# A fused attention layer on one core: the endings' rows read from chunk 12 on, and the shift rows' chain started two half steps earlier

## The chip, the core and the metric

The kernel runs on one core of a Trainium2 chip. The metric is device time in microseconds (us) of one execution. Engines are named as in the profile: PE (TensorE), ACT (ScalarE), DVE (VectorE), POOL (GpSimd), and SP (SyncE), which here does nothing but issue every DMA, in program order.

## What is computed

The input x has 8 batches of 2048 tokens with 512 channels, in float32. Cut to what matters:

```
xn   = layernorm(x)
q, k = heads of xn @ Wq.T + bq, xn @ Wk.T + bk       # 8 heads of 8
v    = heads of xn @ Wv.T + bv                       # 8 heads of 64
beta = softmax(leaky(q k^T / sqrt(8), 0.2))          # over 2048 keys
s    = gamma * (beta v) + xn
g    = silu(xn @ W.T + the low-rank term of the top expert)
out  = x + s * g
```

## The kernel before, in words

**Sequences, chunks, half steps.** A block is 512 tokens, so a batch has four blocks n, and the 8 heads make four pairs p. One sequence is one (batch, pair, block of queries): 16 sequences in a batch, 128 in all, with `b, p, n = s // 16, s % 4, (s % 16) // 4`. A sequence goes through 16 chunks of 128 keys. The double loop over s and i in the main part is written out by hand, and one pass of it is called a half step here and written (s,i); there are 2048. In the trace a half step begins with its first matmul of `less_max` (L657).

**What a half step issues.** On PE: `less_max` for one head (L657), two score matmuls of the next chunk (L640), two matmuls of `max_unit` (L586), `less_max` for the other head; then what the scheduler gives, mostly `weigh` (L681) of earlier chunks. On ACT: two exponentials (L669) and two leaky steps (L651). On DVE: one max reduction of `max_unit`, L597, which frees the only PSUM buffer `mx` for the next half step's two L586. On POOL: one addition of exponentials, L701.

**Maxima and shift rows.** The softmax needs each query's maximum before the sequence starts. `max_unit` runs `CH + LEAD` half steps ahead: with LEAD = 9 the last unit of sequence s+1 is issued in (s,6), and the first unit of sequence s+2 in (s,7). After the last one `shift_rows` is put in a queue and goes on by one `yield` in each half step: a reduction m (L603, DVE) in (s,6); two tiny DVE operations big and m (L609, L610) and a chain of six tiny POOL operations (L611 to L616) in (s,7); the transpose cT (L621, DVE), four DMAs to SH (L623) and four DMAs back to the tile shift (L629) in (s,9). The tile is first used in (s+1,0).

**Stacks.** `load_stacks(s+2)`, called in (s,0) to (s,3), reads the keys and queries of sequence s+2: two DMAs `k` (L542) and two `q_sb` (L548). The three key buffers make the `k` DMA wait for the last scores of sequence s-1, so SP issues it around (s-1,13) to (s,0).

**Ending.** When the last values of sequence s have been weighed, `ending(s)` enters the queue: a copy avs (L708); a half step later the reads of the block's rows, gs (L714) and the two halves of xs (L716, L717); then three idle half steps, the denominators dps (L724, L732, L734, L736), the transposed values atp (L741, L743), the addition of xs (L744), and in the next half step L747, L748 and the write of the output (L749). The tiles `dps` and `atp` take the one PSUM buffer `m`, which the background work takes too.

**Background.** Between the `weigh` matmuls runs a list of tasks: `lift_block` of this batch (the gate g, written to GS at L520, after which the block is `lifted`), and `project_block` of the next batch (L338 to L390: eight writes of keys and queries of 128 KB, then XN and XT, 1 MB each). `norm` and `lift_block` have tiny POOL operations too (L309 to L313, L434, L435). In the last batch only `lift_block` is left, and `half_light` takes the place of `half_full`.

**Order.** All engines run their own instructions in program order. SP waits at a DMA until its source and buffer are free, and everything behind waits with it.

Of the kernel before, what the change touches and what calls it, by code (L numbers as in the profile page):

```python
# [8 lines left out]
FP = mybir.dt.float32  # L9
# [12 lines left out]
NT = BLK // 128  # L22
# [10 lines left out]
def fused_layer_kernel(  # L33
# [37 lines left out]
    nc = tc.nc  # L71
    B, M, C = x.shape
# [3 lines left out]
    SEQ = NPAIR * NB  # L76

    xv = x.rearrange("b (n p t) c -> b n p t c", p=128, t=NT)
# [5 lines left out]
    two = ctx.enter_context(tc.tile_pool(name="two", bufs=2))  # L84
# [12 lines left out]
    GS = [tc.dram_tile([NB, 128, NT, C], FP, name=f"GS{b}") for b in range(B)]  # L97
    XN = [tc.dram_tile([NB, 128, NT, C], FP, name=f"XN{b}") for b in range(B)]
# [110 lines left out]
    def set_up_ffn(ul):  # L209

        nc.vector.tensor_scalar_mul(w_sb, w_sb, 0.5)
        yield

        uh = one.tile([128, C], FP, name="hi")
        nc.vector.tensor_scalar_mul(ul, ul, 0.5)
        nc.vector.tensor_tensor(
            uh.bitcast(I32), ul.bitcast(I32), hi_bits.to_broadcast([128, C]), ALU.bitwise_and
        )
        nc.scalar.copy(wu_sb, uh)
        for g in (1, 3):  # L220
            r = slice(32 * g, 32 * g + 32)
            nc.vector.tensor_tensor(wu_sb[r, :], ul[r, :], uh[r, :], ALU.subtract)
# [21 lines left out]
    TINY, SLOW, WAIT, HOLD, FREE, IDLE = 5, 4, 3, 2, 1, 0  # L244
# [4 lines left out]
    def spend(cost):  # L249
        spent[0] += cost  # L250
# [44 lines left out]
    lifted = []  # L295
# [228 lines left out]
    def where(s):  # L524
        return s // SEQ, s % NPAIR, (s % SEQ) // NPAIR
# [28 lines left out]
    def load_values(s):  # L554
        if s >= B * SEQ:
            return
        b, p, n = where(s)
        while b not in valued:
            force()
        vts[s] = two.tile([128, CH, 128], FP, name="v_sb")  # L560
        nc.sync.dma_start(out=vts[s], in_=VS[b][p])
# [37 lines left out]
    def shift_rows(s):  # L599
        if s >= B * SEQ:  # L600
            return
        m = sm.tile([128, 2 * NT, 1], FP, name="m")
        nc.vector.reduce_max(m, mxr.pop(s).rearrange("p e t n -> p (e t) n"), axis=AX.X)  # L603
        yield IDLE

        ml = sm.tile([128, 2 * NT], FP, name="ml")
        c = parts[s % 2][:, 0 : 4 * NT].rearrange("p (i m) -> p i m", i=2)
        big = sm.tile([128, 2 * NT], FP, name="big")
        nc.vector.tensor_scalar(big, m[:, :, 0], 0.0, SLOPE, ALU.min, ALU.mult)  # L609
        nc.vector.tensor_scalar_max(m[:, :, 0], m[:, :, 0], 0.0)  # L610
        nc.gpsimd.tensor_tensor(ml, m[:, :, 0], big, ALU.add)  # L611
        nc.gpsimd.tensor_tensor(big, ml, splitter.to_broadcast([128, 2 * NT]), ALU.mult)
        nc.gpsimd.tensor_tensor(ml, ml, minus_one.to_broadcast([128, 2 * NT]), ALU.mult)
        nc.gpsimd.tensor_tensor(c[:, 1, :], big, ml, ALU.subtract)
        nc.gpsimd.tensor_tensor(c[:, 0, :], big, c[:, 1, :], ALU.subtract)
        nc.gpsimd.tensor_tensor(c[:, 1, :], ml, c[:, 0, :], ALU.subtract)  # L616
        for _ in range(2):
            yield IDLE

        cT = sm.tile([128, 32], FP, name="cT")  # L620
        nc.vector.transpose(cT, parts[s % 2])  # L621
        for q in range(4):
            nc.sync.dma_start(  # L623
                out=SH[s % 2][:, :, :, q, :].rearrange("i e t j -> (i e t) j"),
                in_=cT[32 * q : 32 * q + 4 * NT, :],
            )
        shift = qp.tile([128, BLK], FR, name="shift")
        for g in range(4):
            nc.sync.dma_start(  # L629
                out=shift[STK * g : STK * g + 2, :].bitcast(FP),  # L630
                in_=SH[s % 2][:, g % 2].rearrange("i t q j -> i (t q j)"),
            )
        shifts[s] = shift
# [19 lines left out]
    def less_max(s, i, sc, e):  # L653

        r = rows(i % 2, e)
        r = slice(r.start, r.start + 2)
        nc.tensor.matmul(  # L657
            sc[e],
            lhsT=ones_r[r, :],
            rhs=shifts[s][r, :],  # L660
            start=False,
            stop=True,
            skip_group_check=True,
        )
# [28 lines left out]
    def add_up(s, i, ex):  # L693
# [6 lines left out]
            acc[s] = two.tile([128, 2, BLK], FP, name="acc")  # L700
        nc.gpsimd.tensor_tensor(acc[s], old, ex, ALU.add)  # L701

    def ending(s):

        b, p, n = where(s)
        cols = slice(p * 128, (p + 1) * 128)
        avs = two.tile([128, BLK], FP, name="avs")
        nc.vector.tensor_copy(avs, avt.pop(s))  # L708
        yield IDLE
        sums = acc.pop(s)  # L710
        while (b, n) not in lifted:
            yield IDLE
        gs = two.tile([128, NT, 128], FP, name="gs")
        nc.sync.dma_start(out=gs, in_=GS[b][n][:, :, cols])  # L714
        xs = two.tile([128, 2, NT, 128], FP, name="xs")
        nc.sync.dma_start(out=xs[:, 0], in_=xv[b, n][:, :, cols])  # L716
        nc.sync.dma_start(out=xs[:, 1], in_=XN[b][n][:, :, cols])  # L717
        for _ in range(3):
            yield IDLE
        yield TINY  # L720

        dps = ps_m.tile([128, 2, NT, 32], FP, name="dps2", tag="m")
        for q in range(4):
            nc.tensor.matmul(  # L724
                dps[32 * q : 32 * q + 32],
                lhsT=ones[:, 0:32],
                rhs=sums.rearrange("p e (t q j) -> p e t q j", t=NT, q=4)[:, :, :, q, :],
                start=True,
                stop=True,
            )  # L730
        dv = dps.rearrange("p e t j -> p (e t) j")
        nc.vector.tensor_tensor(dv, dv, diag.unsqueeze(1).to_broadcast([128, 2 * NT, 32]), ALU.mult)  # L732
        rd = sm.tile([128, NT, 2, 1], FP, name="rd")
        nc.vector.reduce_sum(rd.rearrange("p t e o -> p e t o"), dps, axis=AX.X)  # L734
        rd = rd.rearrange("p t e o -> p (t e) o")
        nc.vector.reciprocal(rd, rd)  # L736
        spend(0.5)
        yield TINY
        tp = ps_m.tile([128, NT, 128], FP, name="atp", tag="m")
        for t in range(NT):  # L740
            nc.tensor.transpose(tp[:, t, :], avs[:, t * 128 : (t + 1) * 128], ident)  # L741
        tv = tp.rearrange("p t (e d) -> p (t e) d", e=2)
        nc.vector.tensor_tensor(tv, tv, rd.to_broadcast([128, NT * 2, DV]), ALU.mult)  # L743
        nc.vector.tensor_tensor(tp, tp, xs[:, 1], ALU.add)  # L744
        spend(0.5)
        yield WAIT
        nc.vector.tensor_tensor(tp, tp, gs, ALU.mult)  # L747
        nc.vector.tensor_tensor(gs, tp, xs[:, 0], ALU.add)  # L748
        nc.sync.dma_start(out=ov[b, n][:, :, cols], in_=gs)  # L749
# [25 lines left out]
    def due_at(h):  # L775
        w, t = h * END, 0.0
        for _, _, _, cost, end in tasks:
            w += cost * max(0.0, min(1.0, (h - t) / (end - t)))
            t = end
        return w  # L780
# [39 lines left out]
    def force():  # L820

        j = ahead()[0] if ahead() else 2
        go(j)
# [55 lines left out]

    MUCH, AHEAD = 3, 6.0  # L880

    LEAD = 9
    END = 1.0
    total = B * SEQ * CH

    with tc.manual_schedule():
# [110 lines left out]
        first, late = shift_rows(0), set_up_ffn(ul)  # L997
        units = [(0, u) for u in range(CH)] + [(1, u) for u in range(LEAD)]
        for n in range(1, NB):
# [30 lines left out]
        for s in range(B * SEQ):  # L1030
            for i in range(CH):
                if i <= 3 and s + 2 not in qst and (where(s + 2)[0] in (0, *ready) or i == 3):
                    load_stacks(s + 2)
                if i >= 6 and s + 1 not in vts and (where(s + 1)[0] in valued or i == 13):
                    load_values(s + 1)
                due[0] = due_at(s + (i + 1) / CH)
                u = s * CH + i + CH + LEAD
                nxt = s * CH + i + 1


                less_max(s, i, sc0, 0)
                if nxt < total:
                    sc1 = score(nxt // CH, nxt % CH)
                max_unit(u // CH, u % CH, flip=True)
                less_max(s, i, sc0, 1)
                if u % CH == CH - 1 and u < total:
                    queue[1], state[1] = shift_rows(u // CH), IDLE
                ex = exp(sc0)
                if nxt < total:
                    leaky(sc1)  # L1050
                if s < (B - 1) * SEQ:
                    half_full()
                else:
                    half_light()
                add_up(s, i, ex)
                last.append((s, i, ex))
                sc0 = sc1
        values(len(last))
        for _ in ending(B * SEQ - 1):
            pass  # L1060
# [44 lines left out]
```

## Time and profile before

| | |
|---|---|
| median of three runs | 5637.28 us (5630.33 to 5653.89) |
| the profiled execution's own time | 5619.18 us |
| its span, first to last instruction | 5617.4 us |
| first less_max matmul of (0,0) and of (127,15) | 131.2 us, 5598.6 us |
| busy share of the span: PE, POOL, ACT, DVE | 96%, 85%, 79%, 65% |
| granted PE clock, mean | 0.968 |

The span divides into 131 us before the loop, 5467 us of loop (2.67 us per half step) and 19 us after it. The length of a half step is read in the timeline as the distance between the first L657 matmuls of two half steps. Rows of a wait read: engine and line that waited, what it waited for, total us, times, longest us. The sums below are made against this execution.

### The profile page before, as it was taken

Reading aid. Unit: us, or ns where it says so; the run is one execution under the profiler, and the core shown is the slowest. Engines: PE = TensorE matmul, PEld = TensorE weight load, DVE = VectorE, ACT = ScalarE, POOL = GpSimd, SP = SyncE. Lnnn points to the kernel's source line nnn. Section 1 sums busy time; section 2 is a strip of 40 time slices with the busy share of each in tenths; the row PEclk is TensorE's granted clock in tenths of the full one; section 3 lists DMA queues with packets and bytes.
Section 4 is the critical chain, followed back from the end, with each engine's and each line's share of the span. In section 5 each row is a group of like instructions: output and inputs, shape, how many; then the busy total and the mean of one; then the engine's idle time right before and its main releaser. Section 6 shows DMA issues by size and latency. Waiting matters only on the chain.

```text
span 5617.4 us, 78032 instructions
## 1 busy us (share of the span) xinstructions
PE 5378.9 (96%) x26258; PEld 1999.1 (36%) x26258; DVE 3673.9 (65%) x4988; ACT 4440.7 (79%) x8627; POOL 4779.1 (85%) x2906
## 2 busy tenths in 40 slices
PE   8999999999999999999999999999999999999998
PEld 3333333333333333333333333333333333333332
DVE  5577666766676666667666666666766766645653
ACT  2788878888888878888788887888878888767777
POOL 1789988888888888888888888888888888878878
PEclk9999999999999999999999999999999999979989
DMA  5333432434324343252432434234343333322221
GB/s 197 106 112 121 128 113 88 128 106 147 104 78 142 93 146 95 76 158 91 142 92 83 147 112 130 80 111 131 107 123 99 102 120 122 100 78 78 71 63 61
DMA packets 528264, 615.38 MB, mean 110 GB/s; under 512 B 44092, under 2 KB 438332, under 8 KB 491768
## 3 DMA queue, kind: packets, MB, share of 16 engines
q1 hardware_dynamic: 527864, 610.39, 35.6%
q8 instruction: 209, 3.42, 0.3%
q14 instruction: 191, 1.56, 0.1%
HBM read 407.88 MB, written 202.38 MB: 109 GB/s over the span
## 4 chain that ended last, share of the span: by engine, by line
PE 80%; ACT 8%; DVE 7%; DMA 2%; issue 2%; SPq 1%; POOL 1%; POOLq 0%; ACTq 0%; DVEq 0%
PE av L681 28%; PE sc L657 16%; PE zps L279 9%; PE vps L279 8%; PE mx L586 7%; ACT ex L669 5%; ACT sc L651 2%; PE pps L265 2%; DVE mxr L597 2%; PE qkps L265 2%; PE dps L265 2%; PE dps L724 1%; DMA xs<-XN 1%; PE atp L741 1%; DVE gs L748 1%
## 5 line engine op out<-in xcount | busy, mean ns | idle before, releaser
L701 POOL TENSOR_TENSOR acc<-acc,ex 128x1024 f32<-128x1024 f32 x1792 | 4231.0, 2361 | 301.7 <-ACT ex L669 189.3
L597 DVE TENSOR_REDUCE mxr<-mx 128x2 f32<-128x1024 f32 x2032 | 2480.2, 1221 | 1260.0 <-PE sc L657 1018.5
L669 ACT ACTIVATE ex<-sc 128x512 f32<-128x512 f32 x4096 | 2231.0, 597 | 972.2 <-PE sc L657 829.0
L651 ACT ACTIVATE sc<-sc 128x512 f32<-128x512 f32 x4096 | 2237.7, 593 | 18.9 <-PE sc L640 18.9
L681 PE MATMUL av<-ex,v_sb 128*64 128x512 f32 x8192 | 2149.5, 630 | 11.6 <-DVE avs L708 9.2
L657 PE MATMUL sc<-shift,ones_r 2*128 2x512 f32 x4096 | 1679.7, 463 | 75.5 <-ACT sc L651 66.9
L586 PE MATMUL mx<-k,q_sb 32*128 32x512 f32 x4096 | 1445.4, 454 | 37.0 <-DVE mxr L597 35.9
L657 PEld LDWEIGHTS sc<-shift,ones_r 2*128 2x128 f32 x4096 | 703.6, 187 | 1560.4 <-ACT sc L651 1450.5
L640 PE MATMUL sc<-q_sb,k 32*128 32x512 f32 x4096 | 1037.4, 503 | 0.0
L681 PEld LDWEIGHTS av<-ex,v_sb 128*64 128x64 f32 x8192 | 469.7, 138 | 839.6 <-issue 805.2
L586 PEld LDWEIGHTS mx<-k,q_sb 32*128 32x128 f32 x4096 | 562.2, 188 | 61.2 <-DVE mxr L597 49.4
L279 PE MATMUL zps<-w_sb,xnT 128*128 128x512 f32 (+1 forms) x1120 | 541.0, 597 | 32.7 <-DMA xnT<-XT 14.1
L279 PE MATMUL vps<-wv_sb,xnT 128*128 128x512 f32 x960 | 475.2, 619 | 7.4 <-DVE gs L748 7.2
L701 POOL TENSOR_TENSOR acc<-ex 128x1024 f32<-128x1024 f32 x128 | 301.8, 2358 | 197.3 <-ACT ex L669 197.3
L640 PEld LDWEIGHTS sc<-q_sb,k 32*128 32x128 f32 x4096 | 385.9, 185 | 0.8 <-issue 0.8
L279 PEld LDWEIGHTS zps<-w_sb,xnT 128*128 128x128 f32 x1120 | 187.6, 192 | 270.3 <-issue 247.9
L279 PEld LDWEIGHTS vps<-wv_sb,xnT 128*128 128x128 f32 x960 | 164.0, 189 | 209.7 <-issue 195.9
L518 DVE SCALAR_TENSOR_TENSOR g<-th,zps 128x512 f32<-128x512 f32 x128 | 88.0, 688 | 189.2 <-ACT th L517 189.2
L611 POOL TENSOR_TENSOR ml<-m,big 128x8 f32<-128x8 f32 x128 | 26.2, 205 | 176.6 <-DVE m L610 176.6
L349 DVE TENSOR_TENSOR vb<-vps,bv_sb 128x512 f32<-128x512 f32 x120 | 83.0, 691 | 95.6 <-PE vps L279 95.4
L265 PE MATMUL dps<-xnT,wd_sb 128*128 128x512 f32 (+1 forms) x280 | 139.1, 607 | 0.0
L265 PE MATMUL pps<-xnT,wp_sb 128*128 128x512 f32 (+1 forms) x280 | 130.9, 585 | 5.0 <-DVE gs L748 5.0
(124 smaller groups left out, 2656.7 us busy)
## 6 DMA issues: line engine op xcount, KB each, us to landing
v_sb<-VS SPq DMA_DIRECT2D x127, 1024.0 KB
k<-KS SPq DMA_DIRECT2D x256, 256.0 KB
XN<-xn SPq DMA_DIRECT2D x32, 1024.0 KB
q_sb<-QS SPq DMA_DIRECT2D x256, 128.0 KB
xnT<-XT SPq DMA_DIRECT2D x32, 1024.0 KB
GS<-g SPq DMA_DIRECT2D x32, 1024.0 KB
gs<-GS SPq DMA_DIRECT2D x128, 256.0 KB
xs<-in_x_dram SPq DMA_DIRECT2D x128, 256.0 KB
```

What stands on the lines that cost most here:

```text
L265: nc.tensor.matmul(ps[:, part], lhsT=wt[:, c, :], rhs=xnT[c][:, part], start=(c == 0 and part.start == 0), stop=(c == NC - 1 and part.stop ...
L279: nc.tensor.matmul(ps[:, part], lhsT=xnT[c][:, t * 128 : (t + 1) * 128], rhs=wt[:, c, part], start=(c == 0 and part.start == 0), stop=(c = ...
L349: nc.vector.tensor_tensor(vb[:, :, t, :], ps.rearrange("p (h d) -> p h d", h=NPAIR), bv_sb.rearrange("p (h d) -> p h d", h=NPAIR), ALU.add,)
L518: nc.vector.scalar_tensor_tensor(g[:, t, :], th, 1.0, ps, ALU.add, ALU.mult)
L586: nc.tensor.matmul(parts[e], lhsT=q_sb[r, t * 128 : (t + 1) * 128], rhs=k_sb[r, kb // 2 * BLK : (kb // 2 + 1) * BLK], start=True, stop=True,)
L597: nc.vector.reduce_max(mxr[s][:, :, t, kb : kb + 1], mx, axis=AX.X)
L640: nc.tensor.matmul(sc[e], lhsT=k_sb[r, i // 2 * 128 : (i // 2 + 1) * 128], rhs=q_sb[r, :], start=True, stop=True,)
L651: nc.scalar.activation(sc[e], sc[e], AF.Prelu, alpha=SLOPE)
L657: nc.tensor.matmul(sc[e], lhsT=ones_r[r, :], rhs=shifts[s][r, :], start=False, stop=True, skip_group_check=True,)
L669: nc.scalar.activation(ex[:, e, :], sc[e], AF.Exp, scale=qscale)
L681: nc.tensor.matmul(avt[s][64 * e : 64 * e + DV, :], lhsT=v_sb[:, i, 64 * e : 64 * e + DV], rhs=ex[:, e, :], start=(i == 0), stop=(i == CH ...
L701: nc.gpsimd.tensor_tensor(acc[s], old, ex, ALU.add)
```

## The change

Four edits are made. The reads of an ending (L714 to L717) move into a function of their own, called at the head of the half steps (s,12) to (s,15) as soon as the block is lifted; the ending takes the tiles from it, and where they aren't there it calls the function itself, and idles one half step more than before. `shift_rows` idles four half steps instead of two between the POOL chain and the transpose. One more idle half step stands between the four DMAs to SH and the four back. LEAD is 11 instead of 9, so that all maxima, and with them the start of `shift_rows`, are issued two half steps earlier; before the loop two more units are issued, and the units end two half steps earlier in the last sequences.

```diff
@@ shift_rows
         nc.gpsimd.tensor_tensor(c[:, 1, :], ml, c[:, 0, :], ALU.subtract)
-        for _ in range(2):
+        for _ in range(4):
             yield IDLE
 
         cT = sm.tile([128, 32], FP, name="cT")
...
                 in_=cT[32 * q : 32 * q + 4 * NT, :],
             )
+        yield IDLE
         shift = qp.tile([128, BLK], FR, name="shift")
         for g in range(4):
             nc.sync.dma_start(
@@ new function, ahead of ending
+    reads = {}
+
+    def read_for_ending(s):
+
+        b, p, n = where(s)
+        if s >= B * SEQ or s in reads or (b, n) not in lifted:
+            return
+        cols = slice(p * 128, (p + 1) * 128)
+        gs = two.tile([128, NT, 128], FP, name="gs")
+        nc.sync.dma_start(out=gs, in_=GS[b][n][:, :, cols])
+        xs = two.tile([128, 2, NT, 128], FP, name="xs")
+        nc.sync.dma_start(out=xs[:, 0], in_=xv[b, n][:, :, cols])
+        nc.sync.dma_start(out=xs[:, 1], in_=XN[b][n][:, :, cols])
+        reads[s] = gs, xs
@@ ending
         sums = acc.pop(s)
-        while (b, n) not in lifted:
+        while s not in reads:
+            read_for_ending(s)
             yield IDLE
-        gs = two.tile([128, NT, 128], FP, name="gs")
-        nc.sync.dma_start(out=gs, in_=GS[b][n][:, :, cols])
-        xs = two.tile([128, 2, NT, 128], FP, name="xs")
-        nc.sync.dma_start(out=xs[:, 0], in_=xv[b, n][:, :, cols])
-        nc.sync.dma_start(out=xs[:, 1], in_=XN[b][n][:, :, cols])
+        gs, xs = reads.pop(s)
         for _ in range(3):
             yield IDLE
         yield TINY
@@ schedule
-    LEAD = 9
+    LEAD = 11
...
                     load_values(s + 1)
+                if i >= 12:
+                    read_for_ending(s)
                 due[0] = due_at(s + (i + 1) / CH)
```

## The prediction

> **What bounds the kernel now.** I read the page's busy shares and slices, the waits, the groups of L609, L621 and L744, and then the timeline where the waits cluster.
>
> ```profile
> PE 5378.9 (96%) x26258; PEld 1999.1 (36%) x26258; DVE 3673.9 (65%) x4988; ACT 4440.7 (79%) x8627; POOL 4779.1 (85%) x2906
> PEclk9999999999999999999999999999999999979989
> ```
>
> PE sets the pace: a usual half step is 2.58 us, in which POOL's addition takes 2.36. A gain must come from PE's idle time (240 us of the span) or from its clock (mean 0.968). Who makes PE idle:
>
> ```profile
> PE mx L586 <- DVE mxr L597: 35.9, 20, 3.7
> PE zps L279 <- DMA xnT<-XT: 14.1, 1, 14.1
> DVE atp L744 <- DMA xs<-XN: 25.9, 8, 4.0
> DVE cT L621 <- POOL c L616: 3.8, 1, 3.8
> ```
>
> The third row belongs to the first edit: DVE stood 25.9 us at xs, in 8 of 128 endings. The fourth belongs to the second: the transpose waited for POOL once in 128, in (126,9), where no more maxima are due. So longer idling ahead of it has nothing to save. One xs wait, in (61,8):
>
> ```profile
> 2747.37 0.49 PE L657 MATMUL sc<-shift,ones_r 2*128 2x512 f32 x1
> 2748.96 0.70 DVE L744 TENSOR_TENSOR atp<-atp,xs 128x512 f32<-128x512 f32 x1 [3.33 <-DMA xs<-XN]
> 2750.84 0.79 PE L586 MATMUL mx<-k,q_sb 32*128 32x512 f32 x2 [2.97 <-DVE mxr L597]
> 2751.99 3.68 PE L681 MATMUL av<-ex,v_sb 128*64 128x512 f32 x8
> 2755.60 0.79 PE L657 MATMUL sc<-shift,ones_r 2*128 2x512 f32 x1
> ```
>
> DVE waits 3.33 for xs, its max reduction queues behind, PE idles 2.97, and then eight L681 take 3.68 instead of the usual 1.94: the clock is halved. The half step lasts 8.23. Why xs is late shows in SP's timeline:
>
> ```profile
> 2731.57 1.28 SPq L338 DMA_DIRECT2D KS<-hi  x2
> 2737.90 0.45 SPq L390 DMA_DIRECT2D XT<-xnT  x1
> 2738.39 1.30 SPq L714 DMA_DIRECT2D gs<-GS  x1
> 2741.20 1.81 SPq L717 DMA_DIRECT2D xs<-XN  x1
> ```
>
> The reads sit in (61,4) behind the 3 MB that `project_block` wrote, and are used 7.8 us later. The same happens after sequences 12, 28, 44, 60, 76, 92 and 108; the eighth wait is 0.19.
>
> **Edit 1, the reads at (s,12).** No instruction is added, only SP's order changes. For these seven, block 3 is lifted by (10,14) of its batch, so SP meets the reads around (60,12), ahead of the stacks of (60,13) and of the writes of (61,2), and the data has twelve half steps, some 30 us, to land. What is late next in (61,8) is nothing: the half step then looks like (60,8) and (60,9), 2.54 and 2.71. The seven long half steps, from the L657 starts, are 7.40 and the 4.87 after it, 7.95, 8.33, 8.23, 5.95, 8.89, 8.80: 60.4 us in eight, less 8 x 2.58 = 20.6, is 39.8. A second way: seven 14 us windows around them, and seven one sequence earlier:
>
> ```profile
> sum 98.00, PE 74.75 PEld 25.88 DVE 49.40 ACT 46.98 POOL 61.38; mean PE 10.68 PEld 3.70 DVE 7.06 ACT 6.71 POOL 8.77
> sum 98.00, PE 97.53 PEld 37.47 DVE 82.09 ACT 89.40 POOL 87.58; mean PE 13.93 PEld 5.35 DVE 11.73 ACT 12.77 POOL 12.51
> ```
>
> 22.8 us less PE work, and the clock column (0.76 in five, 0.88, 1.00) withholds 5 x 3.36 + 1.68 = 18.5: together 41. Here a rule differs. The Trainium skill, "TensorE: Matmul & The Clock Gate", section "HAM oscillation — how this bites in real kernels", has the clock drop only after idle gaps over some 3.4 us. Three of the seven gaps are shorter (2.92, 2.97, 3.08); by the page two of the drops wouldn't be there, and 41 - 2 x 3.36 = 34 us would return. The rows show half clock after 2.97 and 3.08 (not after 2.92), and even after the 1.33 of (54,9) below. I take the rows: -40, bounds -34 and -43.
>
> In the first sequence of batches 1 to 6 GS is written at (0,11), so the reads at (0,12) will make SP wait for its landing, up to the 4.0 us of today's row "SPq L714 <- DMA GS<-g". Behind it are the stacks of (0,13), needed some 16 us after their issue: 0.
>
> Where the block isn't lifted by the half steps (s,12) to (s,15) (sequences 0, 112, 116, 120, 124), the ending idles one half step more. PE does other work meanwhile; which background matmul then meets the `m` buffer changes, and such meetings cost 2 to 3 us each now (PE on gs L748, 2.7 at most). Either sign: 0, bounds -5 and +10.
>
> **Edit 2, the chain two half steps earlier.** LEAD 11 puts L603 in (s,4) and L609 to L616 in (s,5). The transpose stays in (s,9), for four idles replace two. The reads of shift come one code step after its writes; SP waits for those to land anyway, and the earliest the tile is used after is 3.4 us. Cost 0, at most 1. Moved: 0.19 + 0.16 + 0.17 = 0.5 us of DVE out of half steps 6 to 8, where most endings add 1.05 (dps) and twice 1.4 (atp, gs). But one of these is not 0.16:
>
> ```profile
> L609 DVE TENSOR_SCALAR big<-m x128: 159/161/1871, 109.4 to 5544.4; 128x8 f32<-128x8 f32 x128
> ```
>
> Its 51.3 us are 128 x 0.16 and 31 more. In (54,7) it runs from 2450.38 to 2452.25, and POOL's addition ends at 2452.22: it is held while POOL adds. L743, L744 and L597 queue behind; PE idles 1.33, and the half step takes 5.65. The Trainium skill, "GPSIMD Engine Reference", section "Key points", has VectorE contend with GpSimd in its 2-port modes. Taken alone, with POOL busy 85%, it would hold L609 nearly always, some 110 x 1.2 = 130 us (an estimate, with half of an addition per hold). The row holds it noticeably in 23 of 128: mostly POOL is done before DVE comes. I take the row.
>
> Held and dear are sequences 3, 6 and 9 of a batch, where `norm` or `lift_block` put tiny operations on POOL in half steps 3 and 4 (1.0 us for a power). Over their three half steps they lose about 1 x 4, 2.4 x 7 and 3.5 x 6, some 42 us. Does moving save this? At half step 5 POOL's addition ends 1.8 to 2.1 us after DVE's reduction in the same 18, against 1.5 to 1.8 at half step 7: they are held again, now for 2 us. DVE's slack from one reduction to the next is 2.58 - 1.22, with what the buffer allows about 1.57 us. Kind 3: 1.86 + 0.17 - 1.57 = 0.5 (was 1). Kind 6: one vb copy (0.69) follows, so 1.3, and a third of the times a clock drop of 1.6: 1.8 (was 2.4). Kind 9: atp (1.4) follows: 2.05 plus a clock drop, 3.1, but the gate's small operations in (9,8) run free, which returns 2.4. Sum: 4 x -0.5, 7 x -0.6, 6 x +0.7: -2. The other sequences lose DVE crowding, at most 0.1 us x 100: -3. Edit 2: -5, bounds -30 and +25.
>
> **Edit 3, the stacks needed two half steps earlier.** The first unit of a sequence moves from (s-2,7) to (s-2,5). From the last q_sb issue to then it is 16.3 us in the median, but 10.1 to 11.6 in the sequences 8 of a batch, and 5.5 once (sequence 8):
>
> ```profile
> 2428.11 2.94 SPq L542 DMA_DIRECT2D k<-KS  x2
> 2431.10 2.65 SPq L548 DMA_DIRECT2D q_sb<-QS  x2
> 2435.11 0.95 SPq L717 DMA_DIRECT2D xs<-XN  x1
> ```
>
> Here the new reads come before `k`, for the writes at (53,12) were issued in half step 11. So q_sb lands when xs lands now. The packets of all seven end at 2442.1, the need is 2443.3 (six places, slack 1.2 to 2.1, and the completion still has to arrive): 0.7 each; sequence 8 waits 2. +6, bounds 0 and 30 (each 3 late with a half clock). SP's own time for the three reads, 1.9 us, is only moved.
>
> **Before and after the loop.** Two units more ahead of it: four L586 at half clock, 1 us. The first shift reads come behind a 1 MB write and delay (0,0) by some 4 us, at no cost: they are covered by the 14.1 us at xnT in (0,3), without which they would cost 4. At the end ACT and POOL bound; nothing returns. +1.
>
> **Sum:** -40 + 0 - 5 + 6 + 1 = -38, on the profiled execution's 5619.18 (5617.4 of span and 2 around it). The median of three stands 18 us above that; the same step from it gives 5637 - 38 = 5599.
>
> **Rivals.** *The gain is given back* (0.20): edit 2 at its upper bound (L609 held at half step 5, a clock drop each time, +30 against my value) and edit 3 at its own (+24): 5599 + 54 = 5653, or a part of each, 5610 to 5653. For it: both slacks are read to a tenth and lie near zero. Against: they need both bad ends.
>
> *Slower: L609 held everywhere* (0.07). In the median POOL's addition ends 0.38 us before DVE's reduction at half step 5. If POOL lagged by 2.4 us more, each of 128 would be held 2.0, over the slack by 0.5, and in the 28 where atp follows by 1.2 more: 64 + 34 = 98, so 5599 + 98 = 5697. It decides from 1.6 us of lag past the reduction. Against: the chain is as far from its predecessor as before (16 half steps), and POOL regains some 0.2 us in each.
>
> *The reads don't come earlier* (0.04): if `lifted` came too late. (10,14) against (12,12) excludes it for the seven; the time would be 5637 + edits 2 and 3, about 5639.
>
> **How the numbers follow.** The forecast has 0.69 and spans 5570 to 5609, of which I leave 0.02 to its upper tail. A difference under 0.5%, 28 us, can't be told from none here. Range: down to 5570, edits 1 and 2 at their lower bounds (-43 - 30 + 6); up into the first rival to 5628, which leaves about 0.2 out. Faster by over 0.5% (below 5609): 0.67. Within: that tail, most of the first rival and the third, 0.24. Slower: the second rival and what is left of the first, 0.09.
>
> **What would show it.** Right: no row "DVE atp L744 <- DMA xs<-XN" above 1 us; no half step over 6 us in the sequences 13; PE on mxr L597 down from 35.9 by about 23; L609 still with maxima near 2 us. Wrong: L609's mean well above 401 ns; a row of L586 waiting for DMA k<-KS or q_sb<-QS of over 10 us; a clock below 0.968.

## The result, and the profile after

| | before | after |
|---|---|---|
| median | 5639.82 us (4 runs, 5630.33 to 5653.89) | 5602.52 us (4 runs, 5587.86 to 5607.18) |
| ratio, 95% interval | | 0.994, 0.9918 to 0.9961 |
| the profiled execution's own time | 5619.18 us | 5602.28 us |
| its span | 5617.4 us | 5600.5 us |
| granted PE clock, mean | 0.968 | 0.961 |

The change takes 37 us off the median; 38 were forecast. The two profiled executions lie only 17 us apart. In a later series before's 19 runs went from 5618 to 5650 us, the short ones at a granted clock of 0.967, the long ones at 0.961: before's profiled execution is one of its quickest. So medians give the size of an effect here, and traces its place.

Line numbers behind the edits are shifted in the changed kernel: `less_max` is L658, `weigh` L682, the accumulation on POOL L702, the endings' reads L713 to L716, the additions of atp L756 and L757, the output L762. First the page, PE's busy share and clock:

```profile
PE 5408.1 (97%) x26258; PEld 2008.9 (36%) x26258; DVE 3678.3 (66%) x4990; ACT 4440.4 (79%) x8627; POOL 4778.7 (85%) x2906
PEclk9999999999999999998989989999999999989988
```

PE is busy for 29 us more although it has as many matmuls and the span is shorter: more of them run at half clock (442 us of the span, where before has 361). The clock column has 8 in three slices in the middle where it had 9. The waits of PE, in total us, times, longest us:

```profile
PE mx L586 <- DVE mxr L597: 11.9, 13, 1.7
PE zps L279 <- DMA xnT<-XT: 7.6, 1, 7.6
PE sc L658 <- DMA shift<-SH: 5.3, 1, 5.3
PE mx L586 <- issue: 2.3, 4, 1.0
PE mx L586 <- DMA q_sb<-QS: 2.0, 2, 1.2
```

DVE's waits have no row for xs any more (it was 25.9), and PE waits 24 us less for mxr. New are a wait of 5.3 us at the first shift rows and small waits for stacks; the wait at xnT in (0,3), which covers delays ahead of it, shrinks from 14.1 to 7.6. The reads of ending 60, whose xs DVE waited for in before, in SP's timeline:

```profile
2716.55 0.56 SPq L713 DMA_DIRECT2D gs<-GS  x1
2718.61 0.90 SPq L716 DMA_DIRECT2D xs<-XN  x1
2721.27 2.15 SPq L542 DMA_DIRECT2D k<-KS  x2
2732.86 1.28 SPq L338 DMA_DIRECT2D KS<-hi  x2
```

xs is issued in (60,12), ahead of the stacks and 14 us ahead of the block's writes, 30 us before (61,8). That half step takes 2.71 us where it took 8.23.

**Where the time went.** I compared the lengths of all 2048 half steps of the two profiled executions. Sequences are counted within their batch here, and (9,7) stands for half step 7 of a batch's sequence 9; sums over batches 1 to 6 (for 13: all seven places).

| part | before | after | difference | forecast |
|---|---|---|---|---|
| sequences 13 (edit 1) | 331.0 | 290.3 | -40.7 | -40 |
| sequences 9 | 265.6 | 306.1 | +40.5 | +4 |
| sequences 6 | 259.1 | 251.8 | -7.3 | -4 for the chain, +4 for the stacks |
| sequences 3 | 253.8 | 251.7 | -2.1 | -2 |

So the reads give what was forecast, and the traces say that sequences 9 give it all back, ten times more than forecast. The medians, 37 us apart, say that it isn't all given back. The experiments take that up. This is sequence 57, from the timeline of after:

```profile
2561.76 4.80 POOL L702 TENSOR_TENSOR acc<-acc,ex 128x1024 f32<-128x1024 f32 x2
2561.86 0.19 DVE L603 TENSOR_REDUCE m<-mxr 128x8 f32<-128x32 f32 x1
2564.43 2.16 DVE L609 TENSOR_SCALAR big<-m 128x8 f32<-128x8 f32 x1
2566.62 0.17 DVE L610 TENSOR_SCALAR m<-m 128x8 f32<-128x8 f32 x1
2566.71 0.69 DVE L756 TENSOR_TENSOR atp<-atp,rd 128x512 f32<-128x512 f32 x1
2567.43 0.70 DVE L757 TENSOR_TENSOR atp<-atp,xs 128x512 f32<-128x512 f32 x1
2568.04 1.22 DVE L597 TENSOR_REDUCE mxr<-mx 128x2 f32<-128x1024 f32 x1
2569.31 0.76 PE L586 MATMUL mx<-k,q_sb 32*128 32x512 f32 x2 [1.70 <-DVE mxr L597]
2570.42 1.98 PE L682 MATMUL av<-ex,v_sb 128*64 128x512 f32 x4
```

L609 starts in (57,5) at the head of POOL's second addition and ends 0.03 us after it, at 2566.59. L610, L756 and L757 queue behind it on DVE, then the max reduction L597, and PE idles 1.70. Then four L682 take 1.98 us, where eight do at full clock. Half steps (57,9) to (57,14) take 3.06, 4.11, 3.06, 3.06, 4.87, 5.08 us; before they took 2.95, 4.11, 2.43, 2.22, 2.82, 2.81. The 30 us from 1.9 us into (57,5) on, from the windows of before and of after (length, then for PE, weight loads, DVE, ACT and POOL the busy us with the number of instructions in brackets, then the granted clock; the last two are DMA):

```profile
2571.70:2601.70 30.00, 26.97 (x131) 10.34 (x130) 22.27 (x39) 22.36 (x45) 28.08 (x19) 0.89 0.14 36
```

```profile
2564.00:2594.00 30.00, 28.30 (x101) 10.41 (x100) 19.60 (x35) 17.92 (x36) 23.87 (x17) 0.59 0.16 45
```

PE is busier, gets 101 instructions done instead of 131, and has a clock of 0.59 instead of 0.89. In before the hold of sequence 9 (1.67 us, at half step 7) was followed by 6.8 us of half clock in each of six batches; in after it is 24 to 31 us in five, 10 in one. The idle gap of PE ahead of it was no shorter in before, 2.29 to 2.31 us in (9,9), against 1.70 to 1.72 in after's (9,7):

```profile
2581.72 0.49 PE L657 MATMUL sc<-shift,ones_r 2*128 2x512 f32 x1 [2.31 <-ACT sc L651]
```

So the length of the gap doesn't tell how long the clock stays low.

### The profile page after: what moved, and what is told of

The parts are those of the page before. It is cut to its first block, busy times and chain, and to the rows that moved or that the text cites. A ratio compares the mean times of both kernels' runs of the same rounds, so it can differ in the third digit from the quotient of the medians.

```text
span 5600.5 us, 78233 instructions
## 1 busy us (share of the span) xinstructions
PE 5408.1 (97%) x26258; PEld 2008.9 (36%) x26258; DVE 3678.3 (66%) x4990; ACT 4440.4 (79%) x8627; POOL 4778.7 (85%) x2906
## 4 chain that ended last, share of the span: by engine, by line
PE 82%; ACT 7%; DVE 6%; issue 2%; DMA 1%; POOL 1%; SPq 0%; POOLq 0%; ACTq 0%; DVEq 0%
PE av L682 30%; PE sc L658 17%; PE zps L279 9%; PE vps L279 8%; PE mx L586 7%; ACT ex L670 4%; PE pps L265 2%; PE qkps L265 2%; PE dps L265 2%; ACT sc L652 2%; DVE mxr L597 2%; PE dps L737 1%; POOL acc L702 1%; PE atp L754 1%; PE gps L446 1%
## 5 line engine op out<-in xcount | busy, mean ns | idle before, releaser
L702 POOL TENSOR_TENSOR acc<-acc,ex 128x1024 f32<-128x1024 f32 x1792 | 4230.5, 2361 | 301.3 <-ACT ex L670 187.2
L597 DVE TENSOR_REDUCE mxr<-mx 128x2 f32<-128x1024 f32 x2030 | 2477.3, 1220 | 1249.9 <-PE sc L658 1017.6
L682 PE MATMUL av<-ex,v_sb 128*64 128x512 f32 x8192 | 2156.8, 632 | 11.6 <-DVE avs L724 9.2
L658 PE MATMUL sc<-shift,ones_r 2*128 2x512 f32 x4096 | 1683.7, 466 | 62.5 <-ACT sc L652 48.5
L586 PE MATMUL mx<-k,q_sb 32*128 32x512 f32 x4096 | 1460.6, 457 | 17.3 <-DVE mxr L597 11.9
L658 PEld LDWEIGHTS sc<-shift,ones_r 2*128 2x128 f32 x4096 | 706.2, 188 | 1555.7 <-ACT sc L652 1455.0
L682 PEld LDWEIGHTS av<-ex,v_sb 128*64 128x64 f32 x8192 | 469.8, 138 | 842.4 <-issue 807.9
L279 PE MATMUL zps<-w_sb,xnT 128*128 128x512 f32 (+1 forms) x1120 | 559.4, 614 | 23.8 <-DVE gs L761 10.5
L586 PEld LDWEIGHTS mx<-k,q_sb 32*128 32x128 f32 x4096 | 568.3, 189 | 38.8 <-DVE mxr L597 20.4
L702 POOL TENSOR_TENSOR acc<-ex 128x1024 f32<-128x1024 f32 x128 | 301.9, 2358 | 211.3 <-ACT ex L670 211.3
L611 POOL TENSOR_TENSOR ml<-m,big 128x8 f32<-128x8 f32 x128 | 26.2, 205 | 133.5 <-DVE m L610 133.5
```

The lines of the kernel that those rows point to most:

```text
L279: nc.tensor.matmul(ps[:, part], lhsT=xnT[c][:, t * 128 : (t + 1) * 128], rhs=wt[:, c, part], start=(c == 0 and part.start == 0), stop=(c = ...
L586: nc.tensor.matmul(parts[e], lhsT=q_sb[r, t * 128 : (t + 1) * 128], rhs=k_sb[r, kb // 2 * BLK : (kb // 2 + 1) * BLK], start=True, stop=True,)
L597: nc.vector.reduce_max(mxr[s][:, :, t, kb : kb + 1], mx, axis=AX.X)
L658: nc.tensor.matmul(sc[e], lhsT=ones_r[r, :], rhs=shifts[s][r, :], start=False, stop=True, skip_group_check=True,)
L682: nc.tensor.matmul(avt[s][64 * e : 64 * e + DV, :], lhsT=v_sb[:, i, 64 * e : 64 * e + DV], rhs=ex[:, e, :], start=(i == 0), stop=(i == CH ...
```

## The experiments

Three theories at the start. **A:** the reads are worth 40 us in sequences 13; the chain's new place gives about as much back in sequences 9, through the held L609 and the long half clock behind it. **B:** the earlier reads themselves disturb sequences 9, and the chain's place is neutral. **C:** the half clock comes from the gate's small matmuls (L446 and on), not from the hold. Medians of e1 to e12 are of five rounds with before run beside them on the same chip, so ratios are what is compared.

| kernel | median us | ratio to before | 95% interval | seq. 9, us each |
|---|---|---|---|---|
| before | 5627 to 5641 | 1 | | 44.3 |
| after | 5602.52 | 0.9940 | 0.9918 to 0.9961 | 51.0 |
| e1 reads alone | 5593.82 | 0.9931 | 0.9906 to 0.9956 | 45.5 |
| e2 chain alone | 5634.92 | 0.9994 | 0.9981 to 1.0007 | 50.8 |
| e3 after, Prelu | 5541.80 | 0.9840 | 0.9815 to 0.9864 | 42.3 |
| e4 reads, Prelu | 5560.72 | 0.9855 | 0.9829 to 0.9882 | 42.0 |
| e5 after, scalar_tensor_tensor | 5602.61 | 0.9938 | 0.9917 to 0.9960 | 50.4 |
| e6 after, Prelu in seq. 9 | 5542.51 | 0.9833 | 0.9811 to 0.9854 | 43.4 |
| e7 LEAD 10 | 5557.81 | 0.9863 | 0.9843 to 0.9883 | 47.4 |
| e8 LEAD 10, Prelu | 5513.42 | 0.9781 | 0.9760 to 0.9801 | 40.9 |
| e9 before, Prelu in seq. 9 | 5627.96 | 1.0001 | 0.9989 to 1.0013 | 41.1 |
| e10 reads, Prelu in seq. 9 | 5577.83 | 0.9916 | 0.9896 to 0.9936 | 41.9 |
| e11 chain, Prelu in seq. 9 | 5597.90 | 0.9937 | 0.9916 to 0.9958 | 45.1 |
| e12 after, accumulating form | 5550.23 | 0.9830 | 0.9790 to 0.9871 | 43.4 |

### The two parts alone

e1 takes the chain back, as the diff against after shows; e2 makes the same three edits the other way on before, and leaves its reads where they were.

```diff
-        for _ in range(4):
+        for _ in range(2):
...
-        yield IDLE
         shift = qp.tile([128, BLK], FR, name="shift")
...
-    LEAD = 11
+    LEAD = 9
```

> The early reads alone; LEAD 9 and the shift chain as before. Theory A (the early reads are worth the 40 us at the seven sequences 13 of a batch, and the chain's earlier place gave back some 40 us in the sequences 9, by L609 held behind GpSimd ahead of atp, and then by a halved clock): 5640 - 41 = about 5599, no xs wait, half steps (9,8) to (9,10) at 4.1, 3.0, 4.1 as in the kernel before, no (9,7) over 3 us. Theory B (the early reads themselves disturb the sequences 9, as other DMA traffic, and the chain's place is neutral): the same 5600, but with (9,7) at 5 to 7 us. The two differ in the half steps, not in the time.

> The earlier chain alone (LEAD 11, four idle half steps, one between SH and shift); the endings read where they did before. Theory A: the xs waits stay (25 us in 7), (9,7) is 5 to 7 us; the profile of the changed kernel against the one before has +40 in the sequences 9, -9 in the sequences 6, +4 before the loop: 5640 + 20 to 45. Theory B: within 10 us of 5640, (9,7) below 3 us.

The reads alone give 0.9931, 39 us of before's median, and sequences 13 take 291.6 us: their part is shown. In e1 half step (9,7) is 2.82 us in all six batches; in e2 it is 4.85 to 5.68 with 20.5 to 27.3 us of half clock behind. So B is out: it is the chain's place that makes the long half steps. But e2's median is 4 us under before, within its interval of no change, where A wanted 20 to 45 more. So either the loss is smaller in most runs than in the profiled one, or the chain gains elsewhere what it loses here. In the waits of e1 the cover at xnT is whole, and mxr has what (6,9) and its like left in before:

```profile
PE zps L279 <- DMA xnT<-XT: 15.4, 1, 15.4
PE mx L586 <- DVE mxr L597: 11.3, 10, 1.4
```

### The held instruction taken away

The chain's leaky ReLU goes to ScalarE as one instruction; L609 to L611 are gone.

```diff
-        nc.vector.tensor_scalar(big, m[:, :, 0], 0.0, SLOPE, ALU.min, ALU.mult)
-        nc.vector.tensor_scalar_max(m[:, :, 0], m[:, :, 0], 0.0)
-        nc.gpsimd.tensor_tensor(ml, m[:, :, 0], big, ALU.add)
+        nc.scalar.activation(ml, m[:, :, 0], AF.Prelu, alpha=SLOPE)
```

e3 does this to after, e4 to the reads alone.

> The changed kernel with the three operations L609 to L611 (min and times 0.2, max, sum, two on DVE and one on POOL) replaced by one leaky step on ACT, which gives the same values. Nothing on DVE can then be held behind POOL in shift_rows. Theory A: (9,7) near 2.8 us, no stall in the sequences 3, 6, 9 but that for the stacks: 5602 - 40 to - 60, about 5550. If the clock is what loses, whatever starts it (theory C: the halved clock in the sequences 9 and 15 comes from the gate's small operations and not from the hold): less than 15 us faster than 5602, with half clock windows of 20 to 30 us still in the sequences 9.

> The early reads alone (LEAD 9) with the same replacement on ACT. Theory A: the holds of the old place (42 us in the sequences 3, 6 and 9) go, so 5599 - 42, about 5555; and since the stacks are needed two half steps later (6 us in the sequences 6) and the start is as before (4 us), some 10 us below the changed kernel with the replacement. Theory C: 5590 to 5600.

Both are far under their parents, by 1.0% (e3 to after) and 0.8% (e4 to e1). C is out as the main cause: the gate's small matmuls are all there in e3, (9,7) is 2.8, and the half clock in the six sequences 9 is down from 150 us to 34. These 34 us (7 to 14 in three of the six) begin at (9,9) or (9,10) with no hold and behind no gap of PE over 0.83 us; what starts them stays open, and C is not excluded for them. What I expected of their order (e4 10 us below e3) did not come; their intervals overlap.

### Only in sequences 9

In e6 the Prelu stands only where the chain runs during a sequence 9 of a batch, 8 of 128 chains.

```diff
-        nc.vector.tensor_scalar(big, m[:, :, 0], 0.0, SLOPE, ALU.min, ALU.mult)
...
+        if s % 16 == 10:
+            nc.scalar.activation(ml, m[:, :, 0], AF.Prelu, alpha=SLOPE)
+        else:
+            nc.vector.tensor_scalar(big, m[:, :, 0], 0.0, SLOPE, ALU.min, ALU.mult)
...
```

> The change, with the chain's leaky ReLU as one Prelu on ScalarE in place of L609 to L611 only for the chains that run during sequences 9 of a batch (9, 25, ..., 121: 8 of 128). Theory A (what the chain's new place costs is the hold in sequence 9 and the half clock after it, six or seven times 6.7 us): it gets most of what the Prelu everywhere gets (60 us): 5555 to 5570, (9,7) at 2.8 us in all of batches 1 to 6. Rival D (the Prelu's 60 us are spread over all chains: the sixteen other holds, GpSimd's 128 fewer adds): 8 of 128 chains give at most 15 us: 5587 or more, though (9,7) is at 2.8.

These 8 chains give all that the 128 give, 60 us of after's median: 0.994 becomes 0.9833. So at this place of the chain the hold in sequence 9 is what is dear, 10 us by the medians for each of the six that after's trace shows there (7.6 by the lengths of sequences 9), and the other 17 holds cost nothing that the time shows. The window of sequence 57 in e6, from the same point of the sequence:

```profile
2548.30:2578.30 30.00, 28.24 (x145) 11.42 (x144) 22.34 (x38) 25.36 (x52) 28.82 (x18) 1.00 0.22 63
```

PE is as busy as in after (28.24 and 28.30) but gets 145 instructions done instead of 101, at a clock of 1.00. Sequence 57 is one of three without any half clock, though. In the other three of the six, e6 still has 14 to 20 us of it, again behind no gap over 0.83 us; this is the same window of sequence 41:

```profile
1877.90:1907.90 30.00, 29.17 (x121) 10.82 (x121) 18.93 (x35) 21.13 (x44) 26.58 (x17) 0.72 0.22 60
```

Taken together, e6 has 51 us of half clock in these six sequences where after has 150. To see what the same hold cost at its old place, and what the chain's place is worth without it, the same edit went into before (e9), the reads alone (e10) and the chain alone (e11).

> The kernel before, with the Prelu in place of L609 to L611 only for the chains that run in sequences 9 (they run at half step 7 there). It gives the price of the hold at its old place. Theory A (the profile of before shows sequence 9 at 44.3 us against 42 with no hold: 2.3 us, seven times, 16 us): 5615 to 5628, and the price at the new place (60 us: 5602 to 5542) is larger by some 40. Rival F (in most of before's runs the hold costs as much as at the new place, and only the profiled run, with a time below nearly all others, shows it small): 5575 to 5590.

> The reads of the change alone (maxima 9 ahead, two half steps, no further one), and the Prelu only for the chains in sequences 9. Theory A: 16 us under the reads alone (5594): 5570 to 5585. Rival F: 50 to 60 us under it: 5535 to 5550.

> The chain of the change alone (maxima 11 ahead, four half steps and one more, reads where they were), and the Prelu only for the chains in sequences 9: what the chain's new place is worth without the hold. The hold's price at the new place, 60 us in the change, comes off the chain alone (5635): 5572 to 5590. It should lie under before with the same Prelu by what the prediction gave the chain, 5 us for the stalls of sequences 3 and 6 less 6 for the stacks, or by up to 20 if the profile's sequences 3 and 6 (14 us less) count in full.

| reads | chain | with the hold in seq. 9 | without it | the hold costs |
|---|---|---|---|---|
| as before | as before | 1 | 1.0001 | 0 (interval -7 to +6 us) |
| early | as before | 0.9931 | 0.9916 | 0.15%, 8 us (not clear of noise) |
| as before | ahead | 0.9994 | 0.9937 | 0.57%, 32 us |
| early | ahead | 0.9940 | 0.9833 | 1.07%, 60 us |

Rival F is out: at its old place the hold costs little or nothing of the time (even less than my 16), at the new one it costs 32 to 60 us; 32 is about half of what I expected of e11. The traces are less clear-cut: without the hold the six sequences 9 are 34 and 46 us shorter at the new place (e11 against e2, e6 against after), but 19 and 21 us shorter at the old one too (e9 against before, e10 against e1). Between before and e9 this is lost elsewhere, 13 us in the last batch and 10 in sequences 13 and 15.

The column without the hold answers e2's riddle. Without the hold the chain's place is worth 0.64% (36 us) on before and 0.83% (47 us) on the reads: much more than the -5 + 6 of the prediction. In the pair of profiled executions e9 and e11, 32 us apart in span, it comes from sequences 6 (262.6 to 250.3 us in six), the first batch (692.2 to 680.5), the last batch (717.4 to 706.0) and sequences 15 (11 us, by less half clock), while sequences 9 of e11 lose 24 us to half clock that begins at (9,10) in four of the six, with no hold. That last piece I didn't take apart.

What sort of gain it is, e3 and e4 show. Where no chain has a hold, the place two half steps ahead makes no clear difference: 0.9840 (e3) and 0.9855 (e4), with overlapping intervals. In e4 the chain is at its old place, and (6,9) takes 2.71 us as in after; e10, which keeps the holds of sequences 6, has 4.35 to 4.39 there. So at the old place it was the holds outside sequences 9, those of sequences 6 among them, that were dear: from e10 to e4 the time falls by 0.6%, with intervals that don't overlap. The chain's move makes those holds cheap and the one in sequence 9 dear.

### What makes L609 wait

e5 keeps the chain's place and its GpSimd part, and writes the two DVE instructions as scalar_tensor_tensor with a constant tile as second operand.

```diff
+    slope_sb = filled("slope_sb", SLOPE)
+    zero_sb = filled("zero_sb", 0.0)
...
-        nc.vector.tensor_scalar(big, m[:, :, 0], 0.0, SLOPE, ALU.min, ALU.mult)
-        nc.vector.tensor_scalar_max(m[:, :, 0], m[:, :, 0], 0.0)
+        nc.vector.scalar_tensor_tensor(
+            big, m[:, :, 0], 0.0, slope_sb.to_broadcast([128, 2 * NT]), ALU.min, ALU.mult
+        )
+        nc.vector.scalar_tensor_tensor(
+            m[:, :, 0], m[:, :, 0], 0.0, zero_sb.to_broadcast([128, 2 * NT]), ALU.max, ALU.add
+        )
```

> The change, with the chain's two tensor_scalar instructions on VectorE (L609, L610) written as scalar_tensor_tensor, which takes a second operand from SBUF; the chain's result, its place and GpSimd's five steps stay. Theory A1 (the hold is one of this kind of instruction: a short tensor_scalar of SBUF operands waits for the running add of GpSimd to end): L609 is never held, none above 0.3 us where the change has 23 of up to 2.19; half step 7 of sequences 9 falls from 5-7 us to about 2.8, the long half clock after it goes, and the time is near that with the Prelu (5542), at 5540 to 5575. Rival A2 (any small VectorE instruction of SBUF operands is held by the add): L609 or L610 stays at up to 2.2 us, (9,7) stays at 5-7 us, the time stays within 10 us of the change's (5602).

A2's numbers came, A1's did not: the new instruction is held as the old one was. Both groups by source line, durations in ns min/median/max, e5's L611 and after's reduction L603, which stands just ahead of it in the chain:

```profile
L611 DVE SCALAR_TENSOR_TENSOR big<-m,slope_sb x128: 156/157/2169, 111.1 to 5535.8; 128x8 f32<-128x8 f32 x128
```

```profile
L603 DVE TENSOR_REDUCE m<-mxr x128: 185/185/189, 106.2 to 5521.1; 128x8 f32<-128x32 f32 x128
L609 DVE TENSOR_SCALAR big<-m x128: 157/160/2189, 112.6 to 5522.2; 128x8 f32<-128x8 f32 x128
```

"Any small DVE instruction" (A2) is too wide, though: L603 reads and writes SBUF too, starts during an addition of POOL, with more than 0.1 us of it to go, in over 100 of 128 cases, and never takes more than 0.189 us. Of all DVE lines of after that run more than 20 times, L609 alone is ever more than 0.1 us above its median. All its 23 holds (longer than 0.25 us) end 0.03 or 0.04 us after POOL's addition does. The Trainium skill, "SBUF — State Buffer", section "Who interferes with whom", says why: GpSimd's port is shared with a VectorE instruction that runs in a 2-port mode or has two SBUF inputs, the later one waits for the whole instruction of the other, and tensor_scalar can be of this sort except in the form that also writes out an accumulator. e5's instruction has two SBUF inputs; my A1 had overlooked that clause. e12 tests the exception:

```diff
+    slope_sb = filled("slope_sb", SLOPE)
+    total_sb = const.tile([128, 1], FP, name="total_sb")
...
-        nc.vector.tensor_scalar(big, m[:, :, 0], 0.0, SLOPE, ALU.min, ALU.mult)
-        nc.vector.tensor_scalar_max(m[:, :, 0], m[:, :, 0], 0.0)
+        nc.vector.tensor_scalar(big, m[:, :, 0], 0.0, 0.0, ALU.min, ALU.add, accum_out=total_sb)
+        nc.vector.tensor_scalar(m[:, :, 0], m[:, :, 0], 0.0, 0.0, ALU.max, ALU.add, accum_out=total_sb)
+        nc.gpsimd.tensor_tensor(big, big, slope_sb.to_broadcast([128, 2 * NT]), ALU.mult)
         nc.gpsimd.tensor_tensor(ml, m[:, :, 0], big, ALU.add)
```

> The change, with the chain's two tensor_scalar on VectorE in the form that also writes out an accumulator (minimum with 0, then maximum with 0, sums into a tile that nothing reads), and the product with 0.2 as one more tiny step on GpSimd; same place, same tile big, read by GpSimd as before. The Trainium skill, page SBUF: State Buffer, has a VectorE instruction share GpSimd's port when it runs in a 2-port mode (tensor_scalar, except in this form) or has two SBUF inputs (the scalar_tensor_tensor tried earlier), and makes it wait for the whole instruction of GpSimd. Theory P (this port): the first of the two is never held, its maximum stays within 0.1 us of its median, (9,7) falls to 2.8 us, and the time comes to 5540 to 5570, the further GpSimd steps costing something. Rival S (it waits for GpSimd by its place or by the tile that it writes, not by its kind): it is held up to 2.2 us in some 23 of 128 as before, (9,7) stays at 5 to 7 us, and the time stays at 5590 to 5620.

```profile
L611 DVE TENSOR_SCALAR_CACHE_REDUCE big<-m x128: 108/151/153, 112.6 to 5476.0; 128x8 f32<-128x8 f32 x128
L612 DVE TENSOR_SCALAR_CACHE_REDUCE m<-m x128: 160/161/163, 112.8 to 5476.1; 128x8 f32<-128x8 f32 x128
```

The maximum is 0.153 us, with 28 of 128 started during an addition (more than 0.1 us before its end); same engine, place, source and tile big. So the kind of instruction decides, as the page has it, and rival S is out; that what the two engines share is a port is the page's word, which no run here shows. The window of sequence 57 has a clock of 1.00 again (in three of the six sequences 9, 14 to 24 us of half clock are left), and the time is that of the Prelu, though DVE and GpSimd have more instructions than in after:

```profile
2546.10:2576.10 30.00, 28.23 (x144) 11.38 (x144) 22.45 (x42) 25.22 (x51) 28.67 (x20) 1.00 0.22 63
```

### One half step less

e7 puts the maxima 10 ahead with three idles, e8 the same with the Prelu in all chains.

```diff
-        for _ in range(4):
+        for _ in range(3):
...
-    LEAD = 11
+    LEAD = 10
```

> The change with the maxima 10 half steps ahead and three half steps between GpSimd's chain and the transpose (the change: 11 and four; before: 9 and two), reads as in the change. The chain of sequence 9 starts at (9,6). Theory A with the phase of GpSimd's add deciding (before: L609 starts 0.7 us into the add at (9,7) and is held 1.65; the change: 0.23 into it at (9,5), held 2.16): (9,6) is between, so the hold is there in some form and the price of sequence 9 between 4 and 45 us, and the stacks of sequence 6 come with half the waits: 5580 to 5600. Rival E (only half step 5, where the ending's gate operations queue behind the held L609, is bad): sequence 9 costs no more than before, and (6,9) is still without its stall: 5570 to 5580.

> The same with 10 and three, and the Prelu on ScalarE in place of L609 to L611 for all chains. Theory A: with no hold the place of the chain matters little; the stack waits of (6,5), 6 us in all, are smaller: 5530 to 5550, at or a little under the Prelu at 11 and four (5542). Rival: the place matters by itself (the transpose nearer to GpSimd's chain waits for it again at (6,9)): 5555 or more.

Both came out quicker than any theory had them. The waits of PE in e7:

```profile
PE zps L279 <- DMA xnT<-XT: 12.4, 1, 12.4
PE mx L586 <- DVE mxr L597: 3.3, 9, 1.4
```

No row of L586 waits for q_sb, none waits for the first shift rows, and mxr is down from 11.9 to 3.3. Half step (6,5) is 2.58 us in all six batches (after: 2.98 to 4.25), and (6,9) 2.53. L609 is still held in 23 cases, 1.91 us in sequence 9, but there (9,7) takes 4.53 instead of 4.87 to 7.06, with 10 to 20 us of half clock. Against after, in batches 1 to 6, sequences 9 are 22 us shorter, sequences 15 9 us, sequences 0 to 2 7 us, 8 and 10 5 us. So one half step of lead is too many: 0.994 becomes 0.9863. Without any hold it is the same (e3 0.984, e8 0.9781); the stack waits of (6,5) are a part of that, and the rest I didn't take apart. e8 is the best version that I ran: 0.9781, 5513.42 us against before's 5640.86 beside it.

## Why the prediction was right

**The number** (5599, measured 5602.5) was right: its large term by its mechanism, the small rest because two errors cancel.

- **Edit 1, -40:** -40.7 in the seven places, and 0.9931 alone. The step was right as written, and so was the choice of the row over the rule of the Trainium skill ("TensorE: Matmul & The Clock Gate", section "HAM oscillation — how this bites in real kernels"), by which 34 us would have come: after, too, shows half clock after an idle gap of 1.70 us.
- **Edit 2, kind 9, +0.7 each:** this is the step that failed. "2.05 plus a clock drop, 3.1" had the hold (2.16) and the queue behind it right, but took the clock drop as about 1 us. Measured is +6.75 each, for the half clock lasts 24 to 31 us. The return of 2.4 us by the gate's operations in (9,8) came (4.08 to 3.06 at half clock; 2.57 in e6 at full clock) and is lost in it; it was put low, for e9's sequences 9, without the hold at its old place, are 3.2 us shorter each. By experiment the dear hold costs 32 us more than at its old place with the old reads, 52 with the new ones.
- **Edit 2, the gains, -9:** too small. Sequences 6 are held as before but lose the stall of (6,9) altogether (4.34 to 5.92 before, 2.7 after), 14 us in six places where about 4 were put. Without the hold of sequence 9, chain and stacks together are worth 36 to 47 us.
- **Sum of edits 2, 3 and the loop's head, +2:** measured -4 (e2, interval -11 to +4) and, on the reads, 5602.5 against 5593.8 with overlapping intervals. Right in sum by luck: both parts were put too small, and they cancel.
- **Edit 3, +6:** (6,5) costs 6.5 us more in six places (4.25, 3.29, 2.98, 3.85, 3.56, 4.05 against 2.58), sequence 8's 1.0 where 2 were put. Right for this trace, and partly by luck: with the same order of reads e6 loses 6.9 us there, e12 1.3 and e5 0.1.
- **The loop's head, +1:** the cover held only in part. The first `less_max` moved from 131.2 to 139.5 us, 8.3 where 5 were put (1 for the units, 4 for the shift reads), (0,0) to (0,2) lost 2.1 more at half clock, (0,3) with its wait at xnT gave back 6.3, and 4.2 are left.
- **The rule on 2-port modes:** I reckoned 130 us from it if every chain met an addition, and took the row. The row was right for the size, and the rule for the mechanism: POOL is mostly idle when L609 starts (26 of 128 start inside an addition with more than 0.1 us of it to go), but those that do are held to its end.
- **The rivals:** "the gain is given back" named the right mechanism, the hold at half step 5 with a clock drop each time, and 30 us above my value for it, where the trace has 36; what it lacked was the gain beside it. Holds everywhere did not come: 23 in after, as before.

## What to carry to other kernels

A short instruction on VectorE that needs GpSimd's port waits for GpSimd's whole instruction. Where GpSimd runs long additions all the time, give such tiny steps to another engine or a form with one SBUF input outside the 2-port modes; here this took 0.994 to 0.983, more than the whole change. A hold's price isn't its length but what stands behind it: at the chain's new place 6 of 23 holds carried all of it, since there an ending's work queued behind the hold and PE ran dry for 1.7 us; at the old place others were the dear ones. And a part that measures as neutral can be a gain and a loss: take the suspected loss away in the parent too, and compare the four.

## What the runs showed of the hardware that I had not expected

- **How long the clock stays low.** After a gap of 1.70 us the clock was half for 24 to 31 us (five of six sequences 9 in after), with PE busy in nearly all of it (28.3 of 30 us in sequence 57); after the 2.3 us of before's sequences 9 it was 6.8 us, and after gaps of about 3 us in before's sequences 13 it was 3.4 to 6.8 us in six of seven. Stretches of 7 to 24 us began behind no gap over 0.83 us (sequences 9 of e3, e6, e11 and e12). So the gap alone neither starts nor sizes them. What does, and what ends such a stretch, stays open; no run was made on it.
- **It differs from run to run.** before's 19 runs, with the same instructions, had clocks of 0.961 to 0.968. In the traces, sequences 15 show half clock of 6.8 to 10.2 us in some batches and 30.7 in others (in e4 twice). A gain of 0.3% is seen only over many runs, and a single trace can hide it.
- **Which VectorE instruction is held.** A tensor_scalar and a scalar_tensor_tensor of 0.16 us took up to 2.19 and 2.17; a tensor_reduce of SBUF operands (0.19) and the accumulating tensor_scalar (0.15) never more than 0.19, started under the same additions. In after, a reciprocal (L749) and a 32x32 transpose (L621) of SBUF operands start under an addition in 84 and 121 of 128 cases and never take more than 0.21.
